# Two taps of a depthwise convolution on ScalarE and accumulating DMAs instead of TensorE, with another instruction order for the layer

## The chip, the cores and the metric

The kernel runs on one core of a Trainium2 chip. It is one program for a network of two layers, with all its arrays in fp32. The metric is the device time of one execution in microseconds. TensorE is called PE in the profile (its weight loads PEld), VectorE DVE, ScalarE ACT, GpSimd POOL, and SyncE, which here only issues DMAs, SP.

## The reference, cut to what matters

The input x has 2 images, 256 channels and 48 by 48 pixels. Layer 0 normalizes x in groups, and adds to it half of a local attention (7 by 7 window, 4 heads) and half of a convolution branch. In that branch each channel goes through a depthwise 3 by 3 convolution, a ReLU and a second depthwise 3 by 3 convolution:

```python
hid = jax.nn.relu(_dwconv(xr, w1))
oc = _dwconv(hid, w2).reshape(b, kc2, C, h, w)
out_conv = jnp.sum(oc * wts.transpose(0, 2, 1, 3, 4), axis=1)
return rate1 * out_att + rate2 * out_conv
```

`xr` holds nine copies of the same x, and `wts` is a softmax over these nine, so its weights add up to 1: the sum is one copy's `oc`, and `Wfc` drops out. What is computed is `rate2 * dwconv(relu(dwconv(x, w1)), w2)`, with nine multiply-adds per pixel and channel in each convolution.

Layer 1 is a state-space scan over the 2 × 2304 tokens and then a mixture of eight experts, two for each token. The change doesn't touch it.

## The kernel before

**Tiling.** Channels lie on the 128 partitions, in two halves h. The normalized image of batch b and half h is the tile `xp` (128 × 48 × 48). The attention goes over 18 blocks of 8 by 16 queries in each batch, so 36 in all; a block's keys are 14 by 22 pixels (308).

**One block** has, for each half: scores on PE (line 779), masked minima on DVE (789), exponentials on ACT (800), after both halves a reciprocal on DVE (855), the division on ACT (806), transposes on PE (813), two copies on ACT (821 and 822), the mix with the values on PE (831), and a sum into x on DVE (838). Its queries come from products on PE (624) that ACT scales (634). Keys come in 5 groups of up to 10 rows for each batch and half: products on PE (668), sums with the position term on DVE (674), and copies on POOL that mirror the borders (681 to 688). Values are products on PE (714), copied by ACT (721), stored to DRAM and spread there into a table (724 to 748) by DMAs of SP's queue, and loaded for each block (863).

**One strip of the convolution** is half an image of one half of the channels: 24 output rows, so 25 rows of the hidden tile `hid` (1200 elements on each partition). There are 8 strips, and two `hid` buffers. In a strip the taps 1 and 7 (above and below) are products on PE with a diagonal matrix of that tap's weights (569), in three parts of 10, 10 and 5 rows; each part takes one of the four PSUM banks that the key, query, value and mix products also use. The middle tap 4 multiplies on DVE and adds that bank in the same instruction (576), one for each part. The six other taps are one DVE multiply-add each over the strip (582). Then ACT applies the ReLU (586), and DVE adds the nine taps of the second convolution into x (592). All of these are one chain, in which each step needs the one before. The diagonal matrices are made once, by four products on POOL (397).

**The order** is not left to the engines. Every step is handed to a planner (`Flow`) with an engine, an estimated cost in ns, the steps that it needs, the buffers that it takes and frees, and a due time (`PACE0` = 8517 ns for each attention block). The planner runs through its own clock: whenever an engine is free, the ready step with the lowest rank goes next, where the rank is the due time, less the remaining chain of the same due time, less an offset for the kind of step from the table `LEAD0`. The instructions are then issued in the planned order on each engine, and an engine works them in that order: an instruction that must wait holds up those behind it. POOL's instructions are also chained in planned order. The scan and the experts are planned after this layer in the same way or written out in order; their instructions stand behind those of layer 0 on each engine.

The rank, and the offsets of the kinds that the prediction speaks of (before), are:

```python
return {k: o["due"] - tail[k] - self.lead.get(self.kind(k), 0) for k, o in self.ops.items()}, after
...
"c0": 29457, "c1": -218, "c2": -60266, ... "exps": -769, ... "ka": -5442, "kb": -6880, "kk":
-10968, ... "qp": 69, ... "v": 35518,
```

Here c0 is the product of taps 1 and 7, c1 the first convolution, c2 the second, kk, ka and kb are the product, sum and border of the keys, qp the queries' product, v the values' product, and exps the exponentials.

Of the kernel before, what the change touches and what calls it, by code (L numbers as in the profile page):

```python
# [50 lines left out]
KG = 10  # L51
VR = 16
CR = 24
# [175 lines left out]
class Kernel:  # L229
# [104 lines left out]
    def layer0(self, ctx):  # L334


        nc, ins = self.nc, self.ins
        self.ps, self.used_banks = self.pool("ps", 1, ctx, space=bass.MemoryType.PSUM), []
        wts = self.pool("l0w", 1, ctx)
        room = dict(bank=4, banks=2, q=2, prob=3, pt=4, val=3, vout=2, hid=2, place=2)  # L340
        self.begin_flow(self.pool("att", 1, ctx), room, self.PACE0, self.LEAD0)
        self.kp = [wts.tile([P, HP, HP], F32, name=f"kp{h}") for h in range(NH)]
        self.xp = {(b, h): wts.tile([P, H, W], F32, name=f"xp{b}{h}") for b in range(B) for h in range(NH)}
        self.prepare(wts)
        self.scale_weights()
        for b in range(B):
            self.group_norm(b)
            for g in range(-(-H // KG)):
                self.keys(b, g)
            for rb in range(NRB):  # L350
                self.queries(b, rb)
            for pair in range(N // (2 * P)):
                self.values(b, pair)
            self.convolutions(b)
            for i in range(NBQ):
                self.block(b * NBQ + i)
        self.run_flow()
# [5 lines left out]
    def prepare(self, wts):  # L363

        nc, ins, v, r = self.nc, self.ins, self.v, self.r
        l0 = self.l0 = {}

        def new(name, *shape):
            l0[name] = wts.tile([P, *shape], F32, name=name)
            return l0[name]  # L370

        wp = wts.tile([1, 2, P], F32, name="wp")
        pos = wts.tile([1, 2, HP], F32, name="pos")
        line = self.line = wts.tile([P, 2, W], F32, name="line")
# [4 lines left out]
        for key, cost in (("cst", 9500), ("vec", 9000), ("wp", 8500), ("Wk", 9500), ("Wq", 10500), ("Wv", 11500),  # L379
                          ("win", 22000)):  # L380
            self.arrival((key, 0), cost)
        vec = nc.vector
# [7 lines left out]

        self.op(0, ("bv1", 0), "DVE", 220, lambda: vec.tensor_scalar(
            new("bv1", NH), v["bv"], r["rate1"], None, ALU.mult), ("vec", 0))
        new("diag", NH, 2, P)
        for h in range(NH):
            def diag(h=h):
                for i, k in enumerate((1, 7)):
                    nc.gpsimd.tensor_scalar(
                        l0["diag"][:, h, i, :], self.ident, v["w1"][:, 9 * h + k : 9 * h + k + 1], None, ALU.mult
                    )

            self.op(h, ("diag", h), "POOL", 1000, diag, ("vec", 0), ("cst", 0))
        self.op(0, ("wv1", 0), "POOL", 1600, lambda: nc.gpsimd.tensor_scalar(
            l0["Wv"], l0["Wv"], r["rate1"], None, ALU.mult), ("vec", 0), ("Wv", 0))

# [131 lines left out]
    def convolutions(self, b):  # L536


        nc, T = self.nc, self.tiles
        strips = H // CR  # L540

        taps = sorted(range(9), key=lambda k: k != 4)

        def tap(rows, o, i, k):

            di, dj = k // 3 - 1, k % 3 - 1
            r0, r1 = max(rows[0], -di), min(rows[1], H - di)
            c0, c1 = max(0, -dj), min(W, W - dj)
            (to, first), (of, begin) = o, i
            return (to[:, r0 - first : r1 - first, c0:c1],  # L550
                    of[:, r0 + di - begin : r1 + di - begin, c0 + dj : c1 + dj])

        for n in range(NH * strips):
            h, s = divmod(n, strips)
            key, top = (b, h, s), s * CR
            w1 = self.v["w1"][:, 9 * h : 9 * h + 9]
            due = b * NBQ + NBQ / (NH * strips) * (n + 1)
            rows = (max(0, top - 1), min(H, top + CR + 1))

            def hidden(key=key, rows=rows):  # L560
                return T["hid", key], rows[0]


            def product(part, h=h, key=key):
                ps = self.bank_for(("c", (key, part[0])))[:, : (part[1] - part[0]) * W]
                ps = ps.rearrange("p (r c) -> p r c", c=W)
                for i, k in enumerate((7, 1) if part[1] < H else (1, 7)):
                    dst, src = tap(part, (ps, part[0]), (self.xp[b, h], 0), k)
                    nc.tensor.matmul(dst, lhsT=self.l0["diag"][:, h, k // 7, :], rhs=src, start=i == 0, stop=i == 1)

            def middle(part, h=h, w=w1, key=key, rows=rows, hidden=hidden):
                if part[0] == rows[0]:
                    self.large_tile("hid", key, [P, CR + 1, W])
                ps = T["bank", ("c", (key, part[0]))][:, : (part[1] - part[0]) * W]
                dst, src = tap(part, hidden(), (self.xp[b, h], 0), 4)
                nc.vector.scalar_tensor_tensor(
                    dst, src, w[:, 4:5], ps.rearrange("p (r c) -> p r c", c=W), ALU.mult, ALU.add
                )

            def mac1(k, h=h, w=w1, rows=rows, hidden=hidden):  # L580
                dst, src = tap(rows, hidden(), (self.xp[b, h], 0), k)
                nc.vector.scalar_tensor_tensor(dst, src, w[:, k : k + 1], dst, ALU.mult, ALU.add)  # L582

            def relu(key=key, rows=rows):
                t = T["hid", key][:, : rows[1] - rows[0], :]
                nc.scalar.activation(t, t, AF.Relu)  # L586

            def mac2(k, h=h, top=top, hidden=hidden):
                w = self.l0["w2r"][:, 9 * h : 9 * h + 9]
                x = self.x[b][:, h, :].rearrange("p (r c) -> p r c", r=H)  # L590
                dst, src = tap((top, top + CR), (x, 0), hidden(), k)
                nc.vector.scalar_tensor_tensor(dst, src, w[:, k : k + 1], dst, ALU.mult, ALU.add)  # L592

            before = [*self.normalized(b, max(0, rows[0] - 1), min(H, rows[1] + 1)), ("vec", 0)]
            parts = [(r, min(r + KG, rows[1])) for r in range(rows[0], rows[1], KG)]
            for part in parts:
                at, n = (key, part[0]), (part[1] - part[0]) * W
                self.op(due, ("c0", at), "PE", 4 * 403 * n // 480, partial(product, part), *before, ("diag", h),
                        takes=[("bank", ("c", at))])
                self.op(due, ("c1", (at, 4)), "DVE", 140 + 550 * n // 480, partial(middle, part), ("c0", at),  # L600
                        ("c1", ((key, rows[0]), 4)) if part != parts[0] else None,
                        takes=[] if part != parts[0] else [("hid", key)], uses=[("bank", ("c", at))])
            before = [("c1", ((key, part[0]), 4)) for part in parts]
            for k in (0, 2, 3, 5, 6, 8):
                self.op(due, ("c1", (key, k)), "DVE", 1440, partial(mac1, k), *before)
                before = [("c1", (key, k))]
            self.op(due, ("relu", key), "ACT", 1200, relu, *before)
            before = [("relu", key), ("w2r", 0), *self.normalized(b, 0, H)]
            for i, k in enumerate(taps):
                self.op(due, ("c2", (key, k)), "DVE", 1385, partial(mac2, k), *before, uses=[("hid", key)] if i == 8 else [])  # L610
                before = [("c2", (key, k))]

    def queries(self, b, rb):

# [143 lines left out]
    def block(self, c):  # L758
# [109 lines left out]

    PACE0 = 8517
    LEAD0 = {  # L870
        "Wk": -7803, "Wq": -9183, "Wv": -248, "add": 20723, "bkp": -358, "bq8": -4877, "bv1": 4646,
        "c0": 29457, "c1": -218, "c2": -60266, "copy": 5955, "cst": -8105, "diag": 5635, "divide":
        390, "exps": -769, "ga": -2817, "gneg": -12669, "gs": 8830, "ka": -5442, "kb": -6880, "kk":
        -10968, "least": -25345, "line": 9393, "mix": -34165, "qp": 69, "rden": 2736, "relu": 9009,
        "rstd": 15955, "score": 5, "sw": 7450, "v": 35518, "val": -168, "vc": 39943, "ve": -18754,
        "vec": 9550, "vs": 9164, "vt": -3270, "w2r": 17239, "win": -3276, "winw": 261, "woutc":
        25877, "woutd": -19078, "woute": -2982, "woutt": -7577, "woutw": 8787, "wv1": -2323, "x":
        -12051, "xp": -20423,
    }


# [1484 lines left out]
```

## Time and profile before

| | us |
|---|---|
| Median of three runs (lowest, highest) | 1293.67 (1291.54, 1295.15) |
| The profiled execution's own time | 1295.8 |
| Its span, from the first instruction to the last | 1294.0 |
| Layer 0: last sum into x begins | 321.1 |
| First exponential of the attention | 49.4 |

The three stages of the span, by the busy time of each engine in microseconds:

| Stage | Length | PE | DVE | ACT | POOL |
|---|---|---|---|---|---|
| 0 to 322, layer 0 | 322 | 296.6 | 288.6 | 246.9 | 72.9 |
| 322 to 770, scan and first experts | 448 | 433.1 | 347.1 | 364.9 | 361.1 |
| 770 to 1294, experts and results | 524 | 502.8 | 289.2 | 180.9 | 123.7 |

The profile shows one execution. A line of groups gives the source line, the engine, the operation, the output and input tiles, how often it ran, its busy time, the mean of one in ns, and the idle time of the engine just before with what ended it. A line of waits gives who waited for whom, the total in us, how often, and the longest. A line of stretches gives for each engine its busy time and number of instructions in that stretch, and then the granted PE clock (1.00 is full), the DMA engines' busy share and their GB/s. A line of the timeline gives start and duration in us. Matmul ends are modelled, so a busy PE is not PE at its peak.

### The profile page before, as it was taken

Reading aid. Unit: us, or ns where it says so; the run is one execution under the profiler, and the core shown is the slowest. Engines: PE = TensorE matmul, PEld = TensorE weight load, DVE = VectorE, ACT = ScalarE, POOL = GpSimd, SP = SyncE. Lnnn points to the kernel's source line nnn. Section 1 sums busy time; section 2 is a strip of 40 time slices with the busy share of each in tenths; the row PEclk is TensorE's granted clock in tenths of the full one; section 3 lists DMA queues with packets and bytes.
Section 4 is the critical chain, followed back from the end, with each engine's and each line's share of the span. In section 5 each row is a group of like instructions: output and inputs, shape, how many; then the busy total and the mean of one; then the engine's idle time right before and its main releaser. Section 6 shows DMA issues by size and latency. Waiting matters only on the chain. (4 is left out here: it accounts for less than half of the span.)

```text
span 1294.0 us, 23558 instructions
## 1 busy us (share of the span) xinstructions
PE 1232.5 (95%) x8048; PEld 983.4 (76%) x8048; DVE 924.8 (71%) x2425; ACT 792.7 (61%) x1954; POOL 557.6 (43%) x769
## 2 busy tenths in 40 slices
PE   4999999998799999999999997999999999999995
PEld 3566766665567777777777786999999999999994
DVE  5899999999577887879797745555654665566442
ACT  2598978898799888789697552333333333333342
POOL 4411230210357878999889963212121212221220
PEclk9999999999799999999999998999999999999998
DMA  7331322211132234333636238657667667666756
GB/s 283 126 104 41 100 92 76 80 49 41 43 107 89 91 116 120 116 114 120 187 117 186 64 133 278 184 169 254 203 221 236 192 198 228 235 188 199 233 178 208
DMA packets 101658, 194.12 MB, mean 150 GB/s; under 512 B 10635, under 2 KB 82652, under 8 KB 96604
## 3 DMA queue, kind: packets, MB, share of 16 engines
q1 hardware_dynamic: 85020, 168.51, 38.3%
q0 software_dynamic: 14400, 19.74, 7.8%
q10 hardware_dynamic: 2116, 4.33, 1.0%
q8 instruction: 66, 1.08, 0.3%
q14 instruction: 56, 0.46, 0.1%
HBM read 154.24 MB, written 43.23 MB: 153 GB/s over the span
## 5 line engine op out<-in xcount | busy, mean ns | idle before, releaser
L2095 POOL DMA_INDIRECT acc<-ey,token x70 | 108.7, 1552 | 368.5 <-ACT ey L2094 312.1
L2085 PE MATMUL bank<-ext,wt 128*128 128x256 f32 (+1 forms) x1152 | 241.3, 368 | 0.0
L2089 ACT ACTIVATE hid<-bank,bt 128x256 f32<-128x256 f32 (+1 forms) x288 | 132.3, 461 | 170.7 <-PE bank L2085 166.5
L2085 PEld LDWEIGHTS bank<-ext,wt 128*128 128x128 f32 x1152 | 207.0, 190 | 25.0
L681 POOL COPY kp<-kp 128x10 f32<-128x10 f32 (+1 forms) x60 | 24.9, 415 | 179.4 <-DVE kp L674 179.4
L592 DVE SCALAR_TENSOR_TENSOR x<-hid,w2r,x 128x1128 f32<-128x1128 f32 (+3 forms) x72 | 99.9, 1392 | 0.4 <-ACT hid L586 0.2
L2128 PE MATMUL po<-ts,ss 128*128 128x128 f32 x768 | 96.2, 275 | 0.0
L916 PE MATMUL bank<-xn,win 128*128 128x387 f32 x240 | 92.7, 510 | 2.1 <-ACT t L999 2.1
L1129 DVE SCALAR_TENSOR_TENSOR xc<-bank,vec,xc 128x384 f32<-128x384 f32 x144 | 86.6, 610 | 8.4 <-ACT xc L1118 8.1
L2128 PEld LDWEIGHTS po<-ts,ss 128*128 128x128 f32 x768 | 90.9, 192 | 0.0
L1345 ACT ACTIVATE mt<-mt,cum 128x128 f32<-128x128 f32 x288 | 87.8, 393 | 1.7 <-DMA mt<-decays 1.7
L800 ACT ACTIVATE prob<-prob,top 128x308 f32<-128x308 f32 x144 | 78.3, 552 | 16.0 <-DVE top L789 15.6
L1679 POOL DMA_INDIRECT xs<-u,rows x72 | 72.9, 1012 | 17.4 <-issue 14.7
L2132 ACT COPY u<-po 128x128 f32<-128x128 f32 x32 | 8.5, 266 | 114.2 <-PE po L2128 114.2
L2072 DVE TENSOR_TENSOR ss<-hid 128x512 f32<-128x512 f32 x32 | 22.1, 691 | 70.6 <-ACT hid L2089 70.6
L1451 PE MATMUL bank<-wout,y 128*128 128x264 f32 x288 | 72.0, 396 | 0.1
L916 PE MATMUL zbank<-xn,win 128*128 128x384 f32 x192 | 71.2, 492 | 0.5 <-ACT z L1247 0.3
L806 ACT ACTIVATE prob<-prob,rden 128x308 f32<-128x308 f32 x144 | 67.7, 550 | 3.7 <-DVE rden L855 3.7
L582 DVE SCALAR_TENSOR_TENSOR hid<-xp,vec,hid 128x1175 f32<-128x1175 f32 (+1 forms) x48 | 68.4, 1425 | 0.1
L2128 PE MATMUL po<-wt,hid 128*128 128x128 f32 x496 | 65.5, 275 | 0.0
L789 DVE CUSTOM_DVE_ANT_0 prob<-banks,cst 128x308 f32<-128x308 f32 x144 | 61.7, 471 | 3.9 <-PE banks L779 3.6
L916 PEld LDWEIGHTS bank<-xn,win 128*128 128x128 f32 x240 | 42.5, 195 | 24.8 <-issue 3.9
(334 smaller groups left out, 2989.6 us busy)
## 6 DMA issues: line engine op xcount, KB each, us to landing
wt<-in_We SPq DMA_DIRECT2D x36, 2048.0 KB
mt<-decays SPq DMA_DIRECT2D x36, 512.0 KB
ex<-xs SPq DMA_DIRECT2D x36, 265.0 KB
rd<-decays SPq DMA_DIRECT2D x68, 128.0 KB
val<-vtab SPq DMA_DIRECT2D x72, 110.0 KB
bt<-in_We SPq DMA_DIRECT2D x36, 136.0 KB
vraster<-vout SPq DMA_DIRECT2D x18, 256.0 KB
acc<-x SPq DMA_DIRECT2D x36, 128.0 KB
```

What stands on the lines that cost most here:

```text
L582: nc.vector.scalar_tensor_tensor(dst, src, w[:, k : k + 1], dst, ALU.mult, ALU.add)
L592: nc.vector.scalar_tensor_tensor(dst, src, w[:, k : k + 1], dst, ALU.mult, ALU.add)
L800: nc.scalar.activation(t, t, AF.Exp, bias=T["top", c][:, a : a + 1], scale=-1.0, accum_out=T["den", c][:, a : a + 1])
L916: self.nc.tensor.matmul(ps, lhsT=lhs(k), rhs=rhs(k), start=k == 0, stop=k == NH - 1)
L1129: nc.vector.scalar_tensor_tensor(out(), T["bank", ("cv", at)][:, i : i + TB], wc[:, i : i + 1], out(), ALU.mult, ALU.add)
L1345: nc.scalar.activation(t, t, AF.Relu, bias=at_s, scale=-1.0)
L1451: nc.tensor.matmul(ps[:, : C + E], lhsT=T["y", c][:, m, :], rhs=self.l1["wout"][:, m, :], start=m == 0, stop=m == NZ - 1,)
L1679: ins = nc.gpsimd.indirect_dma_start(self.xs, bass.IndirectOffsetOnAxis(ap=of("rows")[:, i, q : q + 1], axis=0), T["u2", g][:, i, :], None,)
L2085: nc.tensor.matmul(ps[:, :rows], lhsT=w1[:, k, c * P : (c + 1) * P], rhs=xt[:, k, :], start=k == 0, stop=k == NH - 1,)
L2089: nc.scalar.activation(hid[:, c, :], ps[:, :rows], AF.Gelu, bias=bt[:, c : c + 1])
L2095: put = nc.gpsimd.indirect_dma_start(self.acc, bass.IndirectOffsetOnAxis(ap=token[:, j : j + 1], axis=0), y, None, compute_op=ALU.add)
L2128: nc.tensor.matmul(p[name], lhsT=v[a][:, c], rhs=v[w][:, c], start=c == 0, stop=c == NHC // 2 - 1)
```

## The change

The products of the taps 1 and 7 on PE, the diagonal matrices and the three-part middle tap on DVE are gone. In their place:

- The middle tap is one ACT pass over the whole strip, which writes `hid` (`middle`).
- For each of the taps 1 and 7, ACT multiplies the shifted `xp` by that tap's weights into a tile `ct` (two buffers, shared by all strips), and POOL issues a DMA that adds `ct` into `hid` (`added`). The second add needs the first one landed. The planner is told 1220 ns for the product, 1000 ns for the issue and 6500 ns for the DMA.
- The six other taps on DVE, the ReLU and the second convolution are as before; the first of these taps needs the second add landed.
- The table `LEAD0` has new values for all kinds of steps.

```diff
-        room = dict(bank=4, banks=2, q=2, prob=3, pt=4, val=3, vout=2, hid=2, place=2)
+        room = dict(bank=4, banks=2, q=2, prob=3, pt=4, val=3, vout=2, hid=2, place=2, ct=2)
...
-        new("diag", NH, 2, P)
-        for h in range(NH):
-            def diag(h=h):
-                for i, k in enumerate((1, 7)):
-                    nc.gpsimd.tensor_scalar(
-                        l0["diag"][:, h, i, :], self.ident, v["w1"][:, 9 * h + k : 9 * h + k + 1], None, ALU.mult
-                    )
-
-            self.op(h, ("diag", h), "POOL", 1000, diag, ("vec", 0), ("cst", 0))
...
-            def product(part, h=h, key=key):
...
-                for i, k in enumerate((7, 1) if part[1] < H else (1, 7)):
-                    dst, src = tap(part, (ps, part[0]), (self.xp[b, h], 0), k)
-                    nc.tensor.matmul(dst, lhsT=self.l0["diag"][:, h, k // 7, :], rhs=src, start=i == 0, stop=i == 1)
-
-            def middle(part, h=h, w=w1, key=key, rows=rows, hidden=hidden):
...
-                nc.vector.scalar_tensor_tensor(
-                    dst, src, w[:, 4:5], ps.rearrange("p (r c) -> p r c", c=W), ALU.mult, ALU.add
-                )
+            def middle(h=h, w=w1, key=key, rows=rows, hidden=hidden):
+                self.large_tile("hid", key, [P, CR + 1, W])
+                dst, src = tap(rows, hidden(), (self.xp[b, h], 0), 4)
+                nc.scalar.activation(dst, src, AF.Identity, scale=w[:, 4:5])
...
+            self.op(due, ("c1", (key, 4)), "ACT", 1270, middle, *before, takes=[("hid", key)])
+            last = ("c1", (key, 4))
+            for k in (1, 7):
+                last = self.added(due, ("1", key, k), rows[0], partial(tap, rows, k=k), hidden, lambda h=h: (self.xp[b, h], 0),
+                                  lambda w=w1, k=k: w[:, k : k + 1], before, last)
+            for k in range(9):
+                if k != 4 and k not in (1, 7):
+                    self.op(due, ("c1", (key, k)), "DVE", 1440, partial(mac1, k), last)
+                    last = ("c1", (key, k))
+            self.op(due, ("relu", key), "ACT", 1200, relu, last)
...
+    def added(self, due, key, first, places, out, of, weight, before, last):
+
+        nc, T = self.nc, self.tiles
+
+        def product():
+            t = self.large_tile("ct", key, [P, CR + 1, W])
+            dst, src = places(o=(t, first), i=of())
+            nc.scalar.activation(dst, src, AF.Identity, scale=weight())
+
+        def issue():
+            (dst, _), (t, _) = (places(o=o, i=of()) for o in (out(), (T["ct", key], first)))
+            nc.gpsimd.dma_start(dst.rearrange("p r c -> p (r c)"), t.rearrange("p r c -> p (r c)"), accum_op=ALU.add)
+
+        self.op(due, ("cp", key), "ACT", 1220, product, *before, takes=[("ct", key)])
+        self.op(due, ("ca", key), "POOL", 1000, issue, ("cp", key), last)
+        self.op(due, ("cd", key), "queue", 6500, lambda: None, ("ca", key), uses=[("ct", key)])
+        return "cd", key
...
     LEAD0 = {
-        "Wk": -7803, "Wq": -9183, "Wv": -248, "add": 20723, "bkp": -358, "bq8": -4877, "bv1": 4646,
-        "c0": 29457, "c1": -218, "c2": -60266, "copy": 5955, "cst": -8105, "diag": 5635, "divide":
-        390, "exps": -769, "ga": -2817, "gneg": -12669, "gs": 8830, "ka": -5442, "kb": -6880, "kk":
-        -10968, "least": -25345, "line": 9393, "mix": -34165, "qp": 69, "rden": 2736, "relu": 9009,
-        "rstd": 15955, "score": 5, "sw": 7450, "v": 35518, "val": -168, "vc": 39943, "ve": -18754,
...
+        "Wk": -608717, "Wq": -423146, "Wv": -576838, "add": 12337, "bkp": -1204691, "bq8":
+        509567, "bv1": 198073, "c1": 157090, "c2": 22734, "ca": -382682, "cd": 268233, "copy":
+        670796, "cp": -146034, "cst": 774307, "divide": -15288, "exps": -515294, "ga": 129366,
+        "gneg": 757694, "gs": -145134, "ka": -262495, "kb": 83277, "kk": -127963, "least":
+        327679, "line": 1122162, "mix": -201580, "place": -335279, "q": -88460, "qp": -159987,
+        "rden": 781296, "relu": 484073, "rstd": 260648, "score": 516114, "sw": 77825, "turn":
+        425614, "v": -193332, "val": -449086, "vc": 208515, "ve": 721085, "vec": -527362, "vs":
...
```

More of the change, by code (lines that the diff above doesn't have):

```diff
@@ L561, in hidden @@
                 return T["hid", key], rows[0]
-            def product(part, h=h, key=key):
-                ps = self.bank_for(("c", (key, part[0])))[:, : (part[1] - part[0]) * W]
-                ps = ps.rearrange("p (r c) -> p r c", c=W)
-                for i, k in enumerate((7, 1) if part[1] < H else (1, 7)):
-                    dst, src = tap(part, (ps, part[0]), (self.xp[b, h], 0), k)
-                    nc.tensor.matmul(dst, lhsT=self.l0["diag"][:, h, k // 7, :], rhs=src, start=i == 0, stop=i == 1)
-            def middle(part, h=h, w=w1, key=key, rows=rows, hidden=hidden):
[L572 to L576, printed above, removed]
-                    dst, src, w[:, 4:5], ps.rearrange("p (r c) -> p r c", c=W), ALU.mult, ALU.add
-                )
+            def middle(h=h, w=w1, key=key, rows=rows, hidden=hidden):
+                self.large_tile("hid", key, [P, CR + 1, W])
+                dst, src = tap(rows, hidden(), (self.xp[b, h], 0), 4)
+                nc.scalar.activation(dst, src, AF.Identity, scale=w[:, 4:5])
             def mac1(k, h=h, w=w1, rows=rows, hidden=hidden):
@@ L586, in relu, with strip, mac2 @@
                 nc.scalar.activation(t, t, AF.Relu)
-            def mac2(k, h=h, top=top, hidden=hidden):
+            def strip(h=h, top=top):
+                return self.x[b][:, h, :].rearrange("p (r c) -> p r c", r=H)[:, top : top + CR, :]
+            def mac2(k, h=h, top=top, hidden=hidden, strip=strip):
                 w = self.l0["w2r"][:, 9 * h : 9 * h + 9]
-                x = self.x[b][:, h, :].rearrange("p (r c) -> p r c", r=H)
-                dst, src = tap((top, top + CR), (x, 0), hidden(), k)
+                dst, src = tap((top, top + CR), (strip(), top), hidden(), k)
@@ L592, in mac2 @@
                 nc.vector.scalar_tensor_tensor(dst, src, w[:, k : k + 1], dst, ALU.mult, ALU.add)
             before = [*self.normalized(b, max(0, rows[0] - 1), min(H, rows[1] + 1)), ("vec", 0)]
[L595 to L607, printed above, removed]
+            self.op(due, ("c1", (key, 4)), "ACT", 1270, middle, *before, takes=[("hid", key)])
[3 more added lines that the diff above has]
+                                  lambda w=w1, k=k: w[:, k : k + 1], before, last)
@@ L608, in convolutions @@
+            for k in range(9):
[3 more added lines that the diff above has]
+            self.op(due, ("relu", key), "ACT", 1200, relu, last)
             before = [("relu", key), ("w2r", 0), *self.normalized(b, 0, H)]
-            for i, k in enumerate(taps):
-                self.op(due, ("c2", (key, k)), "DVE", 1385, partial(mac2, k), *before, uses=[("hid", key)] if i == 8 else [])
+            rest = taps
@@ L611, in convolutions @@
+            for i, k in enumerate(rest):
+                self.op(due, ("c2", (key, k)), "DVE", 1385, partial(mac2, k), *before, uses=[("hid", key)] if i == len(rest) - 1 else [])
                 before = [("c2", (key, k))]
+    def added(self, due, key, first, places, out, of, weight, before, last):
[11 more added lines that the diff above has]
+        return "cd", key
@@ L870 @@
     LEAD0 = {
-        "Wk": -7803, "Wq": -9183, "Wv": -248, "add": 20723, "bkp": -358, "bq8": -4877, "bv1": 4646,
-        "c0": 29457, "c1": -218, "c2": -60266, "copy": 5955, "cst": -8105, "diag": 5635, "divide":
-        390, "exps": -769, "ga": -2817, "gneg": -12669, "gs": 8830, "ka": -5442, "kb": -6880, "kk":
-        -10968, "least": -25345, "line": 9393, "mix": -34165, "qp": 69, "rden": 2736, "relu": 9009,
-        "rstd": 15955, "score": 5, "sw": 7450, "v": 35518, "val": -168, "vc": 39943, "ve": -18754,
-        "vec": 9550, "vs": 9164, "vt": -3270, "w2r": 17239, "win": -3276, "winw": 261, "woutc":
-        25877, "woutd": -19078, "woute": -2982, "woutt": -7577, "woutw": 8787, "wv1": -2323, "x":
-        -12051, "xp": -20423,
+        "Wk": -608717, "Wq": -423146, "Wv": -576838, "add": 12337, "bkp": -1204691, "bq8":
[5 more added lines that the diff above has]
+        425614, "v": -193332, "val": -449086, "vc": 208515, "ve": 721085, "vec": -527362, "vs":
+        2099, "vt": 499427, "w2r": -227326, "win": -253557, "winw": -424118, "woutc": -31554,
+        "woutd": -566898, "woute": -177346, "woutt": -313265, "woutw": -250713, "wp": 557948,
+        "wv1": -897086, "x": -112136, "xp": -178890,
     }
```

## The prediction

> **What bounds the kernel now.** The chain of waits that ended last covers only the final 24 us of the span, so it says nothing of the part that is changed. I therefore read busy time by stretches first, with cuts where the attention layer's stages begin and end.
>
> ```profile
> core 0: us, PE busy (x) PEld busy (x) DVE busy (x) ACT busy (x) POOL busy (x), PEclk, DMA share, GB/s
> 20.00:322.00 302.00, 294.37 (x2034) 196.56 (x2035) 278.75 (x590) 244.84 (x682) 65.03 (x162) 1.00 0.27 85
> 20.00:49.30 29.30, 27.81 (x93) 18.72 (x93) 18.98 (x31) 7.50 (x14) 16.18 (x27) 1.00 0.60 204
> 49.30:321.70 272.40, 266.30 (x1942) 177.59 (x1940) 259.55 (x561) 237.34 (x668) 48.56 (x137) 1.00 0.23 72
> 40.00:300.00 260.00, 258.28 (x1808) 170.32 (x1808) 246.67 (x527) 219.28 (x618) 53.92 (x153) 1.00 0.25 79
> 120.00:160.00 40.00, 40.00 (x274) 28.65 (x273) 38.19 (x86) 37.78 (x101) 9.59 (x20) 1.00 0.27 82
> ```
>
> The reader is to see that DVE works 94.9% of 40 to 300 us (246.67 of 260), and ACT 84.3% of it, 94.5% in its best 40 us. PE shows 99%, but its ends are modelled. So the waits come next: who stands idle, and for whom.
>
> ```profile
> engine line waited for: us in total, times, longest us
> ACT prob L800 <- DVE top L789: 15.6, 13, 7.8
> ...
> DVE hid L576 <- PE bank L569: 10.0, 4, 8.4
> ...
> DVE x L838 <- PE bank L831: 5.5, 16, 0.7
> ...
> DVE prob L789 <- PE banks L779: 3.6, 9, 0.8
> ```
>
> DVE has one large wait, 8.41 us before its first convolution instruction at 35.63 us; the others add up to little. ACT's longest (7.8 us) is the one before the first exponential, at 49.36 us. DVE bounds this stage, and ACT is the next limit, some 10 points below. Third, the groups that the change touches, and what a copy on POOL meets behind a long DVE instruction:
>
> ```profile
> L582 DVE SCALAR_TENSOR_TENSOR hid<-xp,vec,hid 128x1175 f32<-128x1175 f32 (+1 forms) x48 | 68.4, 1425 | 0.1
> L569 PE MATMUL bank<-xp,diag 128*128 128x480 f32 (+3 forms) x96 | 36.9, 510 | 0.0
> L576 DVE SCALAR_TENSOR_TENSOR hid<-xp,vec,bank 128x480 f32<-128x480 f32 (+1 forms) x24 | 14.7, 621 | 10.1 <-PE bank L569 10.0
> L586 ACT ACTIVATE hid<-hid 128x1200 f32<-128x1200 f32 x8 | 9.7, 1207 | 0.1
> ```
>
> ```profile
> 43.54 1.35 POOL L681 COPY kp<-kp 128x10 f32<-128x10 f32 x1 [7.63 <-DVE kp L674]
> 44.83 0.20 POOL L683 COPY kp<-kp 128x10 f32<-128x10 f32 x1
> ```
>
> **The change, part by part.** DVE loses the 24 instructions of line 576. Their row has 14.7 us, 613 ns each, and neighbours overlap by some 75 ns in the timeline, so 24 × 538 ns = 12.9 us go. At 94.9% busy that is 13.6 us of stage. The six other taps (line 582) and the nine of the second convolution stay.
>
> PE loses 96 matmuls. Twelve stood back to back in 4.11 us at 33.90, so 32.9 us go. I cost this at nothing, gain nought: DVE, not PE, ended the waits. POOL loses four diagonal products (2.41 us at 12.02); POOL is idle 78% of 20 to 322, so nothing again. Were DVE's cover gone, PE's 33 us would be a gain.
>
> ACT gains 24 passes over a strip of 1152 or 1200 elements. The nearest rows are the ReLU (1207 ns for 1200) and the normalization (1344 ns for 1152); less 80 ns of overlap, 1.13 us each: 27.1 us (27 to 30 by the two rows). They lie beside DVE, but ACT's slack in 49.3 to 321.7 is only 35 us (272.4 − 237.3).
>
> POOL gains 16 accumulating DMAs, two in series per strip, each with three costs that no row of before shows together. Issue: 0.99 us (the row of the scatters to xs) to 1.55 us (the row of the adds to acc). Data, 590 to 614 KB or about 37 KB for each of 16 engines: the scatters moved 22.0 GB/s per engine (5.97 MB in 6.0% of 16 engines' 280 us), the adds to acc 8.7 (7.87 MB in 13.8% of 410 us), hence 1.7 to 4.3 us. Landing: the first load of 384 KB was used 4.41 us after its issue; at 307 GB/s its bytes take 1.28 us, with the other queue's load 2.56 us, so 1.85 to 3.1 us remain. Then the wait behind DVE: the copy above took 1.35 us, not 0.20, beside a line-582 instruction that ran from 43.39 to 44.82; so 0 to 1.15 us. From the product's end to usable data that is 4.5 to 10.1 us. I take 7.6: nearest is the adding row for data (4.3), the low landing (1.85), an issue between the rows (1.3), little wait (0.15). The planner puts 7.5 in its sum, so DVE's order leaves just this room.
>
> The page "SBUF — State Buffer" of the Trainium skill (SBUF: two separate sides) speaks against such DMAs: DVE and GpSimd share a port pair under an exclusive lock, and GpSimd can't write descriptors while DVE holds it. But it names two-port modes, and for two SBUF inputs only a GpSimd instruction that reads SBUF. The copy above fits that; no row shows whether a DMA's descriptors do. Read strictly, 1.15 us on each of 16 would be 18 us lost; read by its exception, none.
>
> The new waits. On POOL an add waits for its product and for the add before it; the border copies of the keys (681 to 688) stand behind it, and the scores (779) wait for them. On ACT the product waits for one of two ct buffers, so for a landing; exponentials and copies stand behind. On DVE the first tap (line 582) waits for the second landing, the minima (789) and sums (838) behind it. SP's queue gets nothing new, but value loads follow the moved value products.
>
> The order. The rank is due − tail − offset, and several new offsets exceed all due times (35 × 8.5 = 298 us). Three consequences can be read by hand. On PE the key products (−128 us) now come before queries (−160) and values (−193); before, values came first and filled 20.5 to 33.9 us. On DVE the convolution's taps beat the key sums (−262). On ACT the exponentials come last. So keys start at 20.5 us: four groups 6.6 us (their row at 40.43), borders 2.4, queries and their scaling 2.3, scores and minimum 1.8: first exponential near 33.5, not 49.4. The first tap comes after two serial DMAs: ACT free at 22.2, two middles and a product 3.6, two times 7.6: 41.0 us, not 38.55. DVE's old gap from 27.2 to 35.6 becomes one to 41 with four key sums (2.7) and three blocks' minima (5.1) in it: 6.0 idle, not 9.3, so 3.3 gained.
>
> **The sum.** The stage ended at 321.7 us. By DVE: 321.7 − 13.6 − 3.3 = 305. By ACT: of the 27.1 us new, 4.5 lie before the attention starts, so 237.3 + 22.6 = 260 us from 33.5: at 94.5% it ends at 308.6, at 93% at 313, at 90% at 322. Two near-full engines that wait for each other won't both hold their best rate; I take 93%, 313 us, 8.7 us gained. What follows (the scan from 322, the experts from 770) keeps its length, the low clock at its start (0.63 in 322 to 340) too. The profiled execution took 1295.8 us (span 1294.0), 2.1 above the median of 1293.67. So 1287.1 by its time, 1285 against the median.
>
> **The rivals.** (1) ACT takes the whole gain: at 90% the stage ends at 322, 1294 us. For it: 90% is above its 87.1% of before over the same stretch. Against it: ACT's waits were mostly for DVE, which now has less to do.
>
> (2) Slower: the adds land late. DVE works in the planned order, so each microsecond past 7.5 stands before a strip's first tap, up to 16 times. The gain of 8.7 is eaten at 0.54 us late, a DMA of 8.1 us. With issue 1.55, wait 1.15, landing 1.85 and data 4.3 it takes 8.9: 1.4 × 16 = 22 us, 1307. For it: the adding row and the copy's wait. Against it: those adds ran in small rows beside a DMA load of 0.67, this stage has 0.27.
>
> (3) Slower: keys are starved. While taps are ready no key sum gets DVE; a strip's 15 taps take 20 us (6 × 1.36 + 9 × 1.31), in which ACT runs dry once the loaded keys' blocks (5.5 us of ACT each) are done. One such hole in each batch, less 10 us of overlap each: 20 us, 1305. It decides once holes exceed 8.7 us. Against it: a strip's serial DMAs leave DVE bubbles for 0.68 us sums.
>
> (4) The gain is fuller: both engines reach 97%, ACT ends at 33.5 + 268 = 301, DVE at 300 (278.75 − 12.9 us at 97%, and 6.0 idle, from 20): about 20 us less, 1274.
>
> **Chances.** Forecast 0.44, (1) 0.16, (2) 0.20, (3) 0.14, (4) 0.06. A difference below 0.3% (3.9 us) can't be told from no change here. Of the forecast 0.41 is faster and 0.03 the same; of (1) 0.11 same, 0.03 faster, 0.02 slower; (2) gives 0.18 slower, 0.02 faster; (3) 0.14 slower; (4) faster. Faster 0.52, same 0.14, slower 0.34. The likeliest's own range is 1277 to 1290. To hold eight in ten, the range reaches from 1274 (rival 4) past rival (2) at 1307 to 1310, leaving out DMAs at their upper bound.
>
> **What would show it.** Right: no line-576 group, 24 new ACT passes of 1.2 us in the stage, DVE and ACT both near 93%, the first exponential near 33 us, the last sum (838) near 313, the later stages as long as before. Wrong: waits of the first taps for a DMA, of over 0.5 us each (rival 2); waits of the scores for border copies and ACT idle in the middle (rival 3); a first exponential still near 49 us.

## The result, and the profile after

The changed kernel takes 1309.95 us (median of four runs, 1306.74 to 1314.38), the kernel before 1292.66 us beside it (1291.54 to 1295.15). The ratio is 1.0133, with a 95% interval of 1.0096 to 1.0170: slower by 17 us, where 1285 and a gain of 8.7 us were forecast. The profiled execution took 1308.12 us, its span is 1306.3.

The time is lost in layer 0. Its last sum into x ends at 336.7 us, before at 321.7. The first expert activation comes at 818.0 instead of 805.5, so the scan gave 2.5 us back, and the experts keep their length. The stretches of the changed kernel, with the same columns as before (the first from the first exponential to the end of the layer):

```profile
core 0: us, PE busy (x) PEld busy (x) DVE busy (x) ACT busy (x) POOL busy (x), PEclk, DMA share, GB/s
34.00:336.00 302.00, 269.17 (x1902) 177.90 (x1900) 259.27 (x542) 260.28 (x694) 76.98 (x144) 0.94 0.41 109
200.00:240.00 40.00, 31.79 (x185) 20.54 (x186) 26.19 (x59) 27.30 (x70) 5.88 (x20) 0.83 0.38 108
280.00:300.00 20.00, 13.48 (x83) 9.22 (x84) 13.99 (x30) 14.12 (x42) 0.00 (x0) 0.78 0.46 131
```

DVE and ACT both come to 86% (259.27 and 260.28 of 302 us), and they fall together, PE with them: 26 and 27 us of the 40 from 200 on. That does not look like one engine becoming the bound. The column PEclk falls too, to 0.94 over the layer and 0.83 and 0.78 in the two shorter stretches; what that is worth is read at e4. The waits of layer 0 name what the engines stand for:

```profile
engine line waited for: us in total, times, longest us
...
ACT pt L818 <- PE banks L810: 23.9, 14, 10.6
PE bank L828 <- DMA val<-vtab: 20.9, 6, 7.1
DVE x L835 <- PE bank L828: 20.9, 7, 7.8
POOL hid L603 <- DMA hid<-ct: 17.1, 3, 7.0
DVE prob L786 <- PE banks L776: 14.3, 20, 3.1
```

The mix (line 828, before 831) waits 20.9 us for the loads of values, in three places, and the sum (835), the copies (818) and all behind them on DVE and ACT wait with it. Before, the largest such row was 0.2 us. Two groups on ACT and one on PE (busy us, mean ns of one, and idle time before with what ended it):

```profile
L599 ACT ACTIVATE ct<-xp,vec 128x1152 f32<-128x1152 f32 (+1 forms) x16 | 20.4, 1279 | 0.1
L557 ACT ACTIVATE hid<-xp,vec 128x1200 f32<-128x1200 f32 x8 | 10.3, 1306 | 0.0
```

```profile
L828 PE MATMUL bank<-pt,val 110*64 110x128 f32 (+1 forms) x864 | 67.6, 299 | 22.3 <-DMA val<-vtab 20.9 <-DVE wout L454 0.5 <-ACT q L631 0.5
```

ACT's 24 new passes take 30.7 us by these rows, 28.8 without the 80 ns in which neighbours overlap. The mix stood idle for 22.3 us, nearly all for loads.

One of the three holes, in the timeline (SPq is SP's DMA queue; the number in brackets is the idle time before an instruction):

```profile
191.88 4.71 SPq L721 DMA_DIRECT2D vraster<-vout  x3
...
199.76 0.51 SPq L731 DMA_DIRECT2D vtab<-vraster  x1
...
209.68 2.04 SPq L743 DMA_DIRECT2D vtab<-vtab  x3
215.40 3.51 SPq L860 DMA_DIRECT2D val<-vtab  x9
217.68 1.12 PE L828 MATMUL bank<-pt,val 110*64 110x128 f32 x8 [7.15 <-DMA val<-vtab]
...
220.61 0.35 DVE L835 SCALAR_TENSOR_TENSOR x<-bank,bv,x 128x128 f32<-128x128 f32 x1 [7.79 <-PE bank L828]
```

A value goes through four transfers one behind the other: stored, spread into the table, its end rows mirrored, loaded. From the first store to the load this takes 23.5 us here (191.88 to 215.40). The planner was told 2.5, 3.5 and 2.8 us for the first three, 8.8 in all. Before, the first such load went out at 47.68 us and the first mix ran at 68.74: 21 us of slack hid what the path really took. Now the first load goes out at 76.88, and the first mix stands 4.5 us before 79.18 for it. From the first store to the first load it is 22.8 us before (24.92 to 47.68) and 22.5 now (54.38 to 76.88): the path is as long as it was, but it begins 29.5 us later, and the mix only 10.4.

### The profile page after: what moved, and what is told of

It is laid out like the page before. It is cut to its first block, busy times and chain, and to the rows that moved or that the text cites. A ratio compares the mean times of both kernels' runs of the same rounds, so it can differ in the third digit from the quotient of the medians.

```text
span 1306.3 us, 23420 instructions
## 1 busy us (share of the span) xinstructions
PE 1218.2 (93%) x7952; PEld 970.0 (74%) x7952; DVE 915.4 (70%) x2401; ACT 815.7 (62%) x1978; POOL 575.1 (44%) x781
## 5 line engine op out<-in xcount | busy, mean ns | idle before, releaser
L573 DVE SCALAR_TENSOR_TENSOR x<-hid,w2r,x 128x1128 f32<-128x1128 f32 (+2 forms) x72 | 99.4, 1388 | 0.3
L828 PE MATMUL bank<-pt,val 110*64 110x128 f32 (+1 forms) x864 | 67.6, 299 | 22.3 <-DMA val<-vtab 20.9
L828 PEld LDWEIGHTS bank<-pt,val 110*64 110x64 f32 (+1 forms) x864 | 50.6, 147 | 42.7 <-issue 24.0
L786 DVE CUSTOM_DVE_ANT_0 prob<-banks,cst 128x308 f32<-128x308 f32 x144 | 62.4, 472 | 14.9 <-PE banks L776 14.3
L603 POOL DMA_DIRECT2D hid<-ct x16 | 14.1, 884 | 132.3 <-ACT hid L557 99.2
L2071 DVE TENSOR_TENSOR ss<-hid 128x512 f32<-128x512 f32 x32 | 22.1, 691 | 70.6 <-ACT hid L2088 70.6
L810 PE MATMUL banks<-cst,prob 128*110 128x128 f32 (+1 forms) x432 | 62.3, 288 | 7.5 <-DVE top L786 7.2
```

The lines of the kernel that those rows point to most:

```text
L828: nc.tensor.matmul(po[j * HD : (j + 1) * HD, :P], lhsT=T["val", c][:nk, i, a * HD : (a + 1) * HD], rhs=T["pt", key][:nk, j, i, :], start=i ...
```

## The experiments

Theory 1: the new order asks for the values just when the planner believes them there, and they come later. Theory 2: the adding DMAs cost the time. Theory 3: engines hold each other up, ScalarE as the new bound or GpSimd against VectorE. Where layer 0 ends (last step that writes x, in the profiled execution) tells more than the total where the computation is cut. Each ratio is to runs of the kernel before beside it; layer ends are of one profile each, and two profiles of the changed kernel itself (after and g2) end the layer 4.0 us apart:

| Run | What it is | Total, us | Ratio to before (95%) | Layer 0 ends |
|---|---|---|---|---|
| before | | 1292.7 | | 321.7 |
| after | | 1310.0 | 1.0133 (1.0096 to 1.0170) | 336.7 |
| e1 | after, measured costs | 1287.6 | 0.9948 (0.9920 to 0.9975) | 314.9 |
| e2 | after, no adds | not comparable | | 320.0 |
| e3 | after, old offsets | 1311.6 | 1.0136 (1.0101 to 1.0171) | 337.5 |
| e4 | after, no wait for the table | 1280.5 | 0.9901 (0.9872 to 0.9930) | 303.3 |
| f1 | after, measured costs, new offsets | 1272.9 | 0.9842 (0.9821 to 0.9863) | 299.4 |
| f2 | before, measured costs | 1300.1 | 1.0053 (1.0034 to 1.0072) | 327.8 |
| f4 | before, no wait for the table | 1294.3 | 1.0006 (0.9992 to 1.0020) | 321.0 |
| f5 | before, measured costs, new offsets | 1292.9 | 0.9992 (0.9977 to 1.0008) | 319.3 |
| f3 | after, gate | 1303.2 | 1.0060 (1.0041 to 1.0080) | 335.9 |
| h1 | the program of f3 again | 1299.6 | 1.0058 (1.0040 to 1.0077) | 330.3 |
| g2 | after, again | 1308.1 | 1.0105 (1.0058 to 1.0151) | 340.7 |
| g1 | after, no adds, no wait for the table | not comparable | | 304.4 |

**e1: the planner's costs of the value path set near the measured ones** (of each line only the step, its queue and its cost in ns).

```diff
-("vs", key), "queue", 2500     ("vt", (b, group)), "queue", 3500
+("vs", key), "queue", 3000     ("vt", (b, group)), "queue", 8000
-("ve", (b, group)), "queue", 2800     ("val", c), "queue", 3000
+("ve", (b, group)), "queue", 6000     ("val", c), "queue", 4000
```

> The changed kernel; only the planner's costs of the value path's transfers are set nearer to the measured ones (store 3.0, spread 8.0, ends 6.0, load 4.0 us instead of 2.5, 3.5, 2.8, 3.0), so the order comes out anew and no work is added or removed. Theory 1 (the new order asks for the value loads just when the planner believes them there, and they land later: three holes of about 23 us in all): the first value product starts well before 51 us or the first mix later, the mix's waits for the value loads (20.9 us) shrink below 8, the attention stage ends 8 to 22 us sooner, 1288 to 1302 in all. Theory 2 (the adding DMAs and what they slow) and theory 3 (ScalarE, or GpSimd and VectorE holding each other up): same work on the same engines, so 1305 to 1315.

Measured: 1287.56 us, just below the range of theory 1, and 0.4 us is all that the mix waits for value loads. (Its first mix still stands 5.8 us, now until a key sum on DVE, line 671, is done.) The first stores go out at 42.9 us instead of 54.4, and the layer ends 21.8 us sooner. With the same work on the same engines this speaks for theory 1. It doesn't tell yet whether the path was late by itself or because the adds slowed it.

**e2: the 16 adding DMAs left out.**

```diff
-nc.gpsimd.dma_start(dst..., t..., accum_op=ALU.add)
+nc.gpsimd.tensor_copy(t[:, :1, :8], t[:, 1:2, :8])
```

> The changed kernel in its own order; the 16 adding DMAs are not issued, a small copy on GpSimd stands in each one's place (taps 1 and 7 of the first convolution are left out). Theory 1: the value path is late by itself, the three holes stay, only the spreads that met an adding DMA get shorter by 2 to 2.5 us (9.6 to 10.0 down to 7.4): 1302 to 1308. Theory 2: the adding DMAs are the cost, so without them the stage ends 15 us or more sooner, 1285 to 1294. Theory 3: unchanged within 3 us.

The total (1333 us) can't be used: other numbers reach the router, and the experts' group (line 2084) runs 1280 times instead of 1152. Layer 0 ends 16.7 us sooner than in the changed kernel, near theory 2's figure; theory 1 had foreseen far less. DVE works the same instructions in the same order in both, so the lag can be read along its queue: 5.8 us by 55 us (54.62 against 48.86), before any mix; nothing in the first hole; 10.8 after the second (220.61 against 209.85), 15.4 after the third (295.97 against 280.58). The same hole in this run:

```profile
185.45 4.71 SPq L721 DMA_DIRECT2D vraster<-vout  x3
...
192.06 0.51 SPq L731 DMA_DIRECT2D vtab<-vraster  x1
...
199.62 2.04 SPq L743 DMA_DIRECT2D vtab<-vtab  x3
205.24 3.51 SPq L860 DMA_DIRECT2D val<-vtab  x9
...
209.85 0.35 DVE L835 SCALAR_TENSOR_TENSOR x<-bank,bv,x 128x128 f32<-128x128 f32 x1 [3.46 <-PE bank L828]
```

Store to load takes 19.8 us instead of 23.5, the spread alone (to the end rows) 7.6 instead of 9.9. So an adding DMA under way slows the value path, but the hole stays, with 3.46 us instead of 7.79. Both theories hold a part. The first 5.8 us are something else (see the gate below).

**e3: the changed convolution with the offsets of the kernel before** (and none for the new kinds; the diff is the table alone).

> The changed convolution (two taps multiplied on ScalarE, added by DMA) with the offsets of the kernel before, and none for the new operations. Theory 1: the values come first again, so the mix's waits for value loads are gone (below 5 us of 20.9); what is left is an order that was not fitted to the new costs: between 1280 and 1300. Theory 2: the adding DMAs cost the same in any order, 1300 or more. Theory 3: the engines' sums are the same as in the changed kernel, so 1303 to 1315.

A miss for theory 1's figure. The mix waits 3.1 us for value loads instead of 20.9, as it said, but the time is 1311.6, where theories 2 and 3 had it: offsets fitted to another convolution leave nine taps of the second convolution over, which run alone at the end, 12.76 us from 324.70. This run shows that early values are not enough; it prices nothing else.

**e4: no load waits for the table.** The end rows are not written and the loads read a weight's rows.

```diff
-nc.sync.dma_start(strips[:, j], strips[:, 2 * PAD - j])
-nc.sync.dma_start(strips[:, PAD + H + j], strips[:, PAD + H - 2 - j])
...
-nc.sync.dma_start(val[:nk, i, :], self.vtab[b, cb, first : first + nk, :])
+nc.sync.dma_start(val[:nk, i, :], ins["W_out"][first % 384 : first % 384 + nk, :])
```

> The changed kernel in its own order of attention; the end rows of the value table are not written and the value loads read rows of a weight instead of the table, so that no load waits for the table (other values are mixed, all else is computed as before). Theory 1: the three holes go, the last sum of the first layer comes near 313 to 318 instead of 336.4: 1285 to 1293. Theories 2 and 3: the loads only hid another bound, and the time stays within 5 us of 1310.

Measured 1280.46 us, 5 us below what theory 1 had said (1285 to 1293). The adds, the order and the number of expert tiles are those of the changed kernel, and the layer ends 33.4 us sooner, at 303.3. The mix in this run:

```profile
L828 PE MATMUL bank<-pt,val 110*64 110x128 f32 (+1 forms) x864 | 62.0, 282 | 3.1 <-DVE x L835 0.8 <-ACT prob L797 0.7 <-DVE wout L454 0.5
```

22.3 us of idle time before it have become 3.1. Read along DVE's queue, the changed kernel lags by 5.4 us at 54.6, by 13.2 after the first hole (87.67 against 74.47), by 14.1 at 148.4 and 26.3 after the second (229.74 against 203.43), by 33.4 after the third. So the holes cost 7.8 + 12.2 + 7.1 = 27.1 us, and the stretch before them 5.4.

Not all of the 27.1 us is the mix's waiting for loads, which comes to 20.3 in the holes (the 20.9 above, less 0.6 at 145 us). Behind each hole PE ran at a lower granted clock: 0.57 in 79 to 87 us, 0.59 in 210 to 225, 0.51 in 291 to 305. In the second, DVE's first sum behind the load lags by 22.1 us (220.61 against 198.48), its reciprocal at 229.23 by 26.2 (against 202.99), and no load is waited for in between. PE's own work shows it, six transposes (line 810) at the low clock and six behind it:

```profile
210.00:225.00 15.00, 6.79 (x39) 5.18 (x38) 7.21 (x11) 4.39 (x13) 0.00 (x0) 0.59 0.24 77
```

```profile
221.77 1.53 PE L810 MATMUL banks<-cst,prob 128*110 128x128 f32 x6
...
226.42 0.82 PE L810 MATMUL banks<-cst,prob 128*110 128x128 f32 x6
```

In e4, with the same order and no such hole, the clock is 0.99 from 34 us to the layer's end, so the lower clock is gone when the holes are.

**f1: the changed convolution, measured costs, and offsets looked for under these costs.** Against the changed kernel only the costs (spread 8.5, ends 6.5, load 4.5, add 5.5 us) and the table differ.

> The changed kernel with the value path's costs set near the measured ones (store 3.0, spread 8.5, ends 6.5, load 4.5 us, the adding DMA's landing 5.5) and new offsets looked for under these costs; same work. Theory 1 (the loss is the value path's late transfers, by an order made with costs too short): waits of the mix for value loads below 5 us, first layer over by 305 to 314 us, 1276 to 1288. Theory 2 (the adding DMAs cost it by themselves) and theory 3 (engines in each other's way): no better than the re-ordered kernel's 1287.6.

1272.88 us, below both kernels and 3 us below the range of theory 1; the layer ends at 299.4, also sooner than it said. The first stores go out at 34.3 us, the first load at 61.4, the first mix at 67.6, and the mixes wait 0.4 us for loads in all. From just behind its first exponential (31.5) to the end of its layer:

```profile
33.00:299.00 266.00, 254.65 (x1897) 167.69 (x1896) 255.69 (x534) 257.04 (x690) 75.37 (x143) 1.00 0.47 123
```

DVE is at 96.1%, ACT at 96.6%: the adds and ScalarE's new passes are all in this run, so theories 2 and 3 fall as the main cause.

**f2: the same four costs in the kernel before** (the diff of e1).

> The kernel before, with the same four costs as in the first experiment (store 3.0, spread 8.0, ends 6.0, load 4.0 us) and nothing else. Theory 1: in its order the values come first and their transfers have slack, so longer costs buy next to nothing: 1290 to 1302. If instead the costs alone, whatever the convolution, are what made the re-ordered kernel fast: 1280 to 1288.

1300.09 us, at the upper end of the first expectation. Measured costs by themselves do not make the kernel before faster, as they did the changed one (e1); the order that comes out of them and of offsets fitted to other costs is worse here.

**f4: the control for e4, its cut in the kernel before.**

> The kernel before in its own order, with the same cut as in the fourth experiment (end rows of the value table not written, value loads read a weight's rows, so that no load waits for the table). Theory 1: before, the value path was not what the mixes waited for, so at most 5 us go: 1288 to 1296. If the path cost the kernel before as much as the changed one (29 us there), the change of order is not to blame: below 1275.

1294.33 us, ratio 1.0006: no change. The same cut that is worth 29.5 us in the changed kernel (1309.95 to 1280.46) is worth nothing in the kernel before. The wait for the table came with the change.

**f5: the control for f1, the convolution of before with offsets looked for in the same way.**

> The convolution of the kernel before, all nine taps as they were, with offsets looked for under the measured costs (store 3.0, spread 8.5, ends 6.5, load 4.5 us) in the same way as for the changed one. If the two moved taps are worth something by themselves, the changed convolution with looked-for offsets stays 5 us or more below this one; if the gain is the order's alone, the two are within 4 us. Expected of this run: 1283 to 1294.

1292.90 us, the same as before. Its stretch from just before the first exponential (43.8):

```profile
43.00:319.00 276.00, 274.22 (x1986) 184.56 (x1984) 263.01 (x565) 238.66 (x673) 66.59 (x139) 1.00 0.28 85
```

DVE is at 95.3% (263.01 of 276), ACT at 86.5%. With an order looked for on each side, the changed convolution is 20.0 us faster (1272.88 against 1292.90). So the two moved taps are worth 20 us with these two orders (others were not tried); the order and costs that came with them took 37 away (1309.95 − 1272.88).

**The gate, two runs, and a repeat.** What are the 5.4 us before the first hole? In the changed kernel's profile the second pair of normalisations (line 515) takes 6.79 us, the first 1.66. A copy on GpSimd that reads the pair's last column was put before its scaling of the W_in rows (line 428):

```diff
+nc.gpsimd.tensor_copy(self.small_tile("gate", 0, [P, 1]), self.xp[1, 0].rearrange("p r c -> p (r c)")[:, N - 1 :])
 nc.gpsimd.tensor_scalar(w, w, v["norm_w"][:, k : k + 1], None, ALU.mult)
```

> The changed kernel in its own order; GpSimd's first scaling of the W_in rows waits (by a copy of one column) until VectorE's second pair of normalisations of the second image is done. In the changed kernel's profile that pair took 6.79 us, where the first took 1.66, and all behind it came 5.4 us later than in the fourth experiment with the same order. If GpSimd's work beside it is the cause and the stall is in most executions: the pair takes 1.7 to 3.5 us, the first layer ends 2 to 6 us sooner, 1303 to 1308. If the stall is an accident of that execution or has another cause: 1309 to 1312.

> As the gate experiment before, but the gate stands ahead of the first scaling of the W_in rows that GpSimd issues, not of the third: there two scalings ran while the second pair of normalisations stood at 6.77 us, and it went on when GpSimd paused at the gate. If GpSimd's tensor work keeps VectorE's normalisation waiting: the pair ends right behind the place operation at about 45, in 3 to 4 us, the first layer ends 2 to 4 us sooner than in the repeat of the changed kernel, 1302 to 1308 in all, and the mix's waits for value loads stay at 19 to 22 us. If not: the pair at 6.8 us again.

> The changed kernel as it is, beside the others on the same chip: 1308 to 1312. Its new profile tells whether the 6.79 us of the second pair of normalisations is there each time: 6 to 7 us if the same order always falls that way, about 1.7 if it was one execution's accident. The waits of the mix for value loads should be 19 to 22 us again.

The second version was meant to put the copy ahead of all scalings, but on GpSimd's queue it stands behind two in both: the two programs are the same, instruction for instruction. As a test of the gate they failed. As two series of one program they say more. The profile of the first:

```profile
41.95 6.77 DVE L515 TENSOR_SCALAR xp<-x,gmean,grstd 128x1152 f32<-128x1152 f32 x2
...
42.17 0.77 POOL L680 COPY kp<-kp 128x10 f32<-128x10 f32 x1
42.88 0.94 POOL L603 DMA_DIRECT2D hid<-ct  x1
43.53 1.16 POOL L654 TENSOR_TENSOR place<-line 128x384 f32<-128x384 f32 x1
44.34 3.76 POOL L428 TENSOR_SCALAR win<-win,vec 128x520 f32<-128x520 f32 x2
48.79 0.19 POOL L428 COPY gate<-xp 128x1 f32<-128x1 f32 x1 [0.68 <-DVE xp L515]
```

and of the second:

```profile
42.09 1.68 DVE L515 TENSOR_SCALAR xp<-x,gmean,grstd 128x1152 f32<-128x1152 f32 x2
...
42.30 0.84 POOL L680 COPY kp<-kp 128x10 f32<-128x10 f32 x1
42.97 1.07 POOL L603 DMA_DIRECT2D hid<-ct  x1
43.92 1.00 POOL L654 TENSOR_TENSOR place<-line 128x384 f32<-128x384 f32 x1
44.73 3.79 POOL L428 TENSOR_SCALAR win<-win,vec 128x520 f32<-128x520 f32 x2
48.48 0.19 POOL L428 COPY gate<-xp 128x1 f32<-128x1 f32 x1
```

In the first DVE's pair stands until 48.72, behind the end of GpSimd's two scalings at 48.10; in the second it is through before they begin. It is not the pause at the gate that lets DVE go on, as I had read it: in the changed kernel, which has no gate, the pair takes as long and ends at 47.95, while GpSimd's scalings run on to 49.39.

```profile
41.16 6.79 DVE L515 TENSOR_SCALAR xp<-x,gmean,grstd 128x1152 f32<-128x1152 f32 x2
...
43.57 5.82 POOL L428 TENSOR_SCALAR win<-win,vec 128x520 f32<-128x520 f32 x3
```

The layer of the two series' profiles ends at 335.9 and 330.3, so the stall is worth about 5.6 us there, near the 5.4 read from e4 (whose pair took 1.68). These two executions took 1312.57 and 1299.70 us; the rest of their difference arises between the layer's end and the first experts and is not explained. The other 12 executions lie between 1297.3 and 1304.9. The repeat of the changed kernel, at 1308.12 us (1302.32 to 1317.08), had the pair at 6.79 again and 21.5 us of waits for value loads. That the program with the gate is faster (medians 1303.17 and 1299.61) because the stall comes less often fits, but with one profile each it is not shown.

**g1: neither adds nor a wait for the table** (the cuts of e2 and e4 together).

> The fourth experiment's cut (no load waits for the value table) with the second's as well (no adding DMAs; taps 1 and 7 left out). Only the end of the first layer counts, since left-out taps change how many expert tiles are computed. If the adding DMAs cost only by way of the value path: the last sum of the first layer within 2 us of the fourth experiment's 303.0. If they cost engines or GpSimd's queue something besides: 4 us or more sooner.

Layer 0 ends at 304.4 us, e4's at 303.3. With the value path out of the way, the adds cost nothing that these two profiles show.

## Why the prediction was wrong

**The step that failed** is the one on the order: "On PE the key products (−128 us) now come before queries (−160) and values (−193); before, values came first", and, of SP's queue, "value loads follow the moved value products". I took the gain from it, the earlier first exponential, and costed the later values at nothing. What hid their transfers before was 21 us of slack between the first load and the first mix, and it went with the move. In its place stand three holes of 27.1 us in all, 20.3 of them waits of the mix for loads; the rest arose behind these waits, where the granted clock was 0.5 to 0.6. With the adds left out, 10.9 of e2's 16.7 us (what is beyond the 5.8 at the start) come from the adds slowing this path; so some 17 us of the 28 after the start (33.4 − 5.4) are the path's own, in this order, and 11 the adds', with one profile for each figure. The transfers' true lengths could be read before: the spread that begins at 31.84 there releases the end rows at 39.26, 7.4 us, where the planner was told 3.5.

**The sum closes.** Forecast end 313, by engines at 93%. Without the holes they do better: e4 ends at 303.3. Add 5.4 for the stalled pair, 27.1 for the holes and 0.9 between them: 336.7, as measured. The three are read from one lag, so they must add up; that they are separate things is shown by h1, where the stall is gone and the holes stay, and e4, where both are gone.

**Right by its steps:**
- The first exponential came at 34.07 (forecast 33.5), line 576 is gone, and the work of ACT from there is 260.3 us (forecast 260). DVE's total busy time is 11.9 us below before's in f1 (924.8 to 912.9), and 14.7 without the 2.8 us of a shorter stall of the same pair that f1 still has; I took 12.9.
- The adding DMA: 5.9 to 7.9 us from issue to the release of the next add (105.53 to 111.42; 128.72 to 136.58), where I took 7.6. The issue took 0.88 us, below my bracket of 0.99 to 1.55.
- Later stages kept their length within 3 us.

**Mis-sized:** 93% for two near-full engines. In the changed kernel it is 86, in f1's order, without the holes, 96. The fuller gain of rival 4 (97% and 1274 us) is near what f1 reached, 1272.9, though with another order than the one forecast.

**The rivals.** The adds did not land late for the taps: no row of the waits has line 561 behind a DMA. Rival 2's 1307 us is near the result by accident; what the adds delayed was another queue's transfers. Keys were not starved: the minima wait for the scores 14.3 us in 20 pieces, 3.1 at most, where one hole of 10 us in each batch was the rival's mechanism. ACT did not take the gain: it is at 96.6% in f1. None of the rivals had the value path in it.

## What to carry to other kernels

When an edit comes with a new order, follow each chain that the order moves to its last consumer, its DMAs by their measured lengths and not by the planner's, and subtract: slack that goes is a cost even where no instruction is added. A change to a planned kernel should be judged with an order fitted to it under true costs, and so should the kernel it is compared with; here the same convolution was 17 us slower than the kernel before in one order, and in another 20 us faster than the old convolution in an order looked for in the same way. A control is worth its run: the cut that gave 29.5 us in one kernel and nothing in the other settled what no trace alone could.

## What was unexpected of the hardware

**One program, two outcomes.** The pair of normalisations took 6.77 us in one execution and 1.68 in another of the same program. The page "SBUF — State Buffer" of the Trainium skill (Who interferes with whom) says that when DVE runs in a two-port mode, which a tensor_scalar can enter, it contends with GpSimd: the one that issues first gets the shared ports for its whole instruction, and the other blocks until then. Here DVE's second instruction, begun at 42.80 us, stood through four instructions of GpSimd in a row, until 48.72, not through one. Which of the two outcomes comes is not explained: in both executions this instruction begins 0.08 us ahead of GpSimd's issue of the add (42.80 and 42.88, 42.89 and 42.97). In my prediction I had weighed only DVE making GpSimd wait.

**An adding DMA slows other transfers, and takes longer than its bytes would suggest.** The spread of values took 9.9 us beside one (the changed kernel) and 7.6 without (e2). For 600 KB the page "DMA: Bandwidth & Descriptors" (Anatomy of one DMA — SWDGE (gpsimd) path) would make an estimate of 3.4 us, 2.0 fixed and the bytes at 436 GB/s; in the three places of the changed kernel where an add waited for the one before, that one took 5.0 to 7.0 after an issue of 0.86 to 0.90 us.

**The issue of such a DMA was not held up by this DVE instruction.** One began at 105.53 us while a line-573 instruction ran from 104.89 to 106.31, and took 0.90 us, near the mean of all 16 (0.88).
